# Router of a conditioned low-rank expert layer: four quarter products of TensorE side by side, gates turned on two column tiles

## The chip, the core and the metric

The kernel runs on one core of a Trainium2 chip. A core has five engines that run side by side and meet at semaphores: TensorE (PE in the profile; its weight loads are a row of their own, PEld), VectorE (DVE), ScalarE (ACT), GpSimd (POOL) and SyncE (SP, which here only issues DMAs). TensorE holds one operand (the weights, `lhsT`) in its array and streams the other (`rhs`) through it; results land in PSUM, 128 partitions by eight banks of 512 float32. The array can be used whole (128x128) or as smaller tiles, chosen by the partitions from which the operands come (rows of the array) and to which the result goes (columns). The metric is the device time of one execution, in microseconds (us). The profile's time is that of one execution taken by the hardware profiler.

## What is computed

`x` is 64 batches of 64 channels by 1024. Each batch picks one of 16 weight matrices (64x64) and mixes its channels by it; the mixed rows (4096 rows of 1024) go through a layer of 64 experts of rank 16, of which each row uses the 16 with the highest router scores. All is float32.

```python
W = weights[condition]                            # (64, 64, 64)
y = jnp.einsum('bct,bcd->bdt', x, W)              # mixed rows
xf = y.reshape(-1, 1024)
scores = xf @ Wr.T                                # (4096, 64)
top_vals, top_idx = jax.lax.top_k(scores, 16)
gates = jax.nn.softmax(top_vals, axis=-1)
G = jnp.zeros((N, K)).at[rows, top_idx].set(gates)
h = jnp.einsum('nd,krd->nkr', xf, A)
out = jnp.einsum('nkr,kdr->nd', h * G[:, :, None], B)
x = x + (out * 2.0).reshape(x.shape)
```

## The kernel before

The 4096 rows are handled in eight groups of 512 rows (`NG = 8`), each of four row tiles of 128 (`TPG = 4`); a row tile holds two batches of 64 rows. Since mixing the channels and multiplying by `A` commute, the kernel first multiplies the unmixed rows by `A` with the router's weights `Wr` appended (the products named `h_...`), and mixes afterwards with the 64x64 matrices `w_st` that GpSimd gathers per batch (`gather`). The mixed, gated result `hb` is multiplied by `B` (the products named `o_...`), and the input is added.

Both large products are done by a scheme with seven products instead of eight per level, two levels deep. The unit of the program's order is a *parent*, one of the seven outer products (p1 to p7); `run` writes one parent's work out by hand: inner products p1, p2, then the previous parent's p3, its own p6, the previous parent's p4, then the hooks `mid`, the operand sums for the next parent, the hooks `late`, then p7 and p5, then the hooks `end`. Each inner product is two matmuls of 272 columns (h) or 256 (o), in the profile four records. Inner products pile up in three PSUM banks a parent, x, y and w; ScalarE copies the pile x out three or four times while it grows (tiles `l_r1`, `l_a`, `l_b` at L601, and L608), and VectorE adds y and w. TensorE may go on with pile x only when ScalarE has copied it.

The first group does not use the inner level (lines L545, 512 columns), and its router scores come another way: `scores_t` (line tile `st`) multiplies `Wr` by the rows, with weights of 64 columns on two column tiles in turn, `turn` (`sp`) turns them, and `scores` mixes them from the tile `zr`. For groups 1 to 7 the scores before mixing are the last 16 columns of each quarter of z.

The router's steps of a group are hooks between products of other work:

- `scores` (L204 to L230): for each row tile i and batch j of it, one 64x64 weight block `ws[g][r, i, :]`, rows and result both on partitions `r`, that is, the upper-left or the lower-right quarter of the array. In group 0 one matmul of 64 columns each (L212, 8 of them), in the others two of 32 columns each (L221, 16). All results go into one PSUM tile `sw`, which one ScalarE copy (L229) takes to `sc`.
- `route_top` (VectorE, top 8 of each row at L243, and the negated maximum), `exps` (ScalarE, L249), `rest` (VectorE, the other 8, the mask, the sum and its reciprocal `inv`).
- `scaled` (L285 to L295): ScalarE multiplies the masked exponentials by `inv` into four tiles `g2`, each 128 rows by 2x64: the gates are written twice, side by side.
- `gates` (L297 to L302): TensorE transposes the four tiles (128x128 each) into the PSUM tile `gp`, and one ScalarE copy of 128x512 takes it to `gg`: experts on partitions, in both halves, rows of the group along the free axis.
- `gated` (L308 to L336): the mixing of h. Per quarter of z, 64 matmuls with 64x64 weights and 64 columns, each on another quarter of the array than the one before, the two row halves into two PSUM tiles `zp`; VectorE multiplies them by `gg` into `hb` (L334).

For groups 1 to 7 `scores` is a `mid` hook of the second parent after the group's last h parent, and `route_top` comes `late` in the same parent. In groups 2 to 6 `scaled` is a `mid` hook and `gates` a `late` hook of one parent, so TensorE has nothing of its own between them. In groups 1 and 7 `gates` is an `end` hook, so p7 and p5 of the parent stand between. In group 0 `scaled` ends one parent, and `gates`, directly followed by `gated`, is the `mid` hook of the next. PSUM tiles come from one pool of eight buffers (`acc`); every parent of groups 1 to 7 takes three, `sw` one, `gp` one, each `gated` two.

Of the kernel before, what the change touches and what calls it, by code (L numbers as in the profile page):

```python
# [9 lines left out]
F32 = mybir.dt.float32  # L10
# [5 lines left out]
P = 128  # L16
# [4 lines left out]
TPG = 4  # L21
CH = 4
HN = TPG * P // 2
HALF = BANK // 2
# [5 lines left out]
def kernel(  # L30
# [26 lines left out]
    nc = tc.nc  # L57
    N, T = x.shape
    B = cond.shape[1]
    C, D = N // B, cw.shape[1]  # L60
    KR = b_t.shape[0] * b_t.shape[3] * b_t.shape[2]
    K = wr_t.shape[2]
# [10 lines left out]
    small = ctx.enter_context(tc.tile_pool(name="small", bufs=2))  # L73
    acc = ctx.enter_context(tc.tile_pool(name="acc", bufs=8, space=PSUM))
# [66 lines left out]
    ident = const.tile([P, P], F32)  # L141
# [9 lines left out]
    ws = {}  # L151
# [17 lines left out]
    gg = blocks.tile([P, TPG * P], F32, name="gg")  # L169


    def scores_t(st):

        g = st["g"]
        s = acc.tile([P, 2, HN], F32, tag="acc", name=f"st_{g}")
        for h in range(2):
            for c in range(2 * CH):
                e = slice((c % 2) * K, (c % 2 + 1) * K)
                nc.tensor.matmul(
                    s[e, h, :],  # L180
                    lhsT=wr_sb[:, c, :],
                    rhs=xq[g, c // CH, h][:, c % CH, :],
                    start=(h == 0 and c < 2),
                    stop=(c >= 2 * CH - 2),
                    skip_group_check=True,
                )
        st_sb = mp0.tile([P, 2, BANK], F32, tag="m", name=f"st_sb_{g}")[:, 0, :]
        nc.scalar.copy(st_sb, s.rearrange("p h n -> p (h n)"))
        st["st"] = st_sb
# [13 lines left out]

    def scores(st):  # L204

        g = st["g"]
        sw = acc.tile([P, TPG, K], F32, tag="acc", name=f"sw_{g}")
        for i in range(TPG):
            for j in range(2):
                r = slice(j * C, (j + 1) * C)  # L210
                if "zr" in st:
                    nc.tensor.matmul(  # L212
                        sw[r, i, :],
                        lhsT=ws[g][r, i, :],
                        rhs=st["zr"][r, i, :],
                        start=True,
                        stop=True,
                    )
                    continue
                for k in range(2):  # L220
                    nc.tensor.matmul(  # L221
                        sw[r, i, ts(k, K // 2)].rearrange("p (d k) -> p d k", d=2),
                        lhsT=ws[g][r, i, :],
                        rhs=halves(st["z"][i // 2, k])[r, i % 2, :, HALF:],
                        start=True,
                        stop=True,
                    )
        scs = small.tile([P, TPG, K], F32, tag="sc", name=f"sc_{g}", bufs=1)
        nc.scalar.copy(scs, sw)  # L229
        st["sc"] = scs  # L230

    def route_top(st):
# [52 lines left out]
    def scaled(st):  # L285
        st["g2"] = []
        for i in range(TPG):
            g2 = small.tile([P, 2, K], F32, tag=f"g2_{i}", name=f"g2_{st['g']}_{i}", bufs=1)
            nc.scalar.activation(
                g2,  # L290
                st["e"][:, i, :].unsqueeze(1).to_broadcast([P, 2, K]),
                AF.Copy,
                scale=st["inv"][:, i : i + 1],
            )
            st["g2"].append(g2)  # L295

    def gates(st):  # L297

        gp = acc.tile([P, TPG, P], F32, tag="acc", name=f"gp_{st['g']}")
        for i in range(TPG):  # L300
            nc.tensor.transpose(gp[:, i, :], st["g2"][i].rearrange("p a k -> p (a k)"), ident)  # L301
        nc.scalar.copy(gg.rearrange("p (i n) -> p i n", n=P), gp)  # L302

    def halves(m):

        return m.rearrange("p s (d k) -> p s d k", d=2)
# [551 lines left out]
    for k, g in (  # L858
# [4 lines left out]
        st = sts[g]  # L863
# [79 lines left out]
    st = sts[0]  # L943
    h, o = st["h"], st["o"]
# [11 lines left out]
    a_sums(2)  # L956
    at(h + 1, "mid", a_sums, 3)
    at(h + 1, "end", scores_t, st)
    at(h + 1, "end", sums, st, "x_sums", "s3")
    at(h + 2, "mid", turn, st)  # L960
    at(h + 2, "mid", a_sums, 4)
    at(h + 2, "end", scores, st)
    for j in ("p1", "p2"):
        at(h + 2, "end", steps_of, first_steps[j], 1)
    at(h + 3, "mid", route_top, st)
    at(h + 3, "mid", sums, st, "x_sums", "s4")
    at(h + 3, "end", exps, st, 0, 1, 2, 3)
    at(h + 4, "mid", rest, st, 0, 1, 2, 3)
    at(h + 4, "end", scaled, st)
    at(h + 4, "end", b_sums, 1)  # L970
    at(h + 5, "mid", gates, st)
    at(h + 5, "mid", gated, st, 0, 0)
    at(h + 5, "end", b_sums, 2)
# [39 lines left out]
    for st in sts[1:]:  # L1013
        n, g = st["h"] + 7, st["g"]
        at(n + 1, "mid", scores, st)
        at(n + 1, "late", route_top, st)
        at(n + 2, "mid", exps, st, 0, 1)
# [20 lines left out]
        for i, (k, when) in enumerate(slots):  # L1038
            at(n + k, when, rest, st, i)
        at(n + scale[0], scale[1], scaled, st)  # L1040
        at(n + turned[0], turned[1], gates, st)
        for (k, when), *quarters in pairs:
            for i, j in quarters:
# [4 lines left out]
    for st in sts:  # L1048
        g, h, o = st["g"], st["h"], st["o"]
# [71 lines left out]
```

## Time and profile before

| what | value |
|---|---|
| median of 3 runs | 781.17 us (780.6 to 781.56) |
| the profiled execution | 780.21 us |
| its span, from first to last instruction | 778.4 us (1.8 us lie around it) |
| granted TensorE clock | 0.999 |
| TensorE busy | 770.6 us, 99% of the span |
| VectorE busy | 623.8 us, 80% |
| ScalarE busy | 184.5 us, 24% |
| GpSimd busy | 73.8 us, 9% |
| mean share of the 16 DMA engines, 300 to 695 us | 0.78 |
| `scores`, groups 1 to 7 (L221): matmul records | 224 |
| `gates`, all groups (L301): matmul records | 32 |
| copy of `sw` to `sc` (L229) | 372 ns, 8 times |
| copy of `gp` to `gg` (L302) | 585 ns, 8 times |

A matmul's record in the profile runs from its start to a modelled end, and neighbours overlap; a float32 product shows as two records, a transpose as one. What a stage costs on TensorE is therefore read from the chain of waits, where each piece begins when the one before it has ended.

### The profile page before, as it was taken

Reading aid. Unit: us, or ns where it says so; the run is one execution under the profiler, and the core shown is the slowest. Engines: PE = TensorE matmul, PEld = TensorE weight load, DVE = VectorE, ACT = ScalarE, POOL = GpSimd, SP = SyncE. Lnnn points to the kernel's source line nnn. Section 1 sums busy time; section 2 is a strip of 40 time slices with the busy share of each in tenths; the row PEclk is TensorE's granted clock in tenths of the full one; section 3 lists DMA queues with packets and bytes.
Section 4 is the critical chain, followed back from the end, with each engine's and each line's share of the span. In section 5 each row is a group of like instructions: output and inputs, shape, how many; then the busy total and the mean of one; then the engine's idle time right before and its main releaser. Section 6 shows DMA issues by size and latency. Waiting matters only on the chain.

```text
span 778.4 us, 14669 instructions
## 1 busy us (share of the span) xinstructions
PE 770.6 (99%) x5348; PEld 610.9 (78%) x5348; DVE 623.8 (80%) x1310; ACT 184.5 (24%) x490; POOL 73.8 (9%) x103
## 2 busy tenths in 40 slices
PE   9999999999999999999999999999999999999997
PEld 4445448888888888887888888888888888888886
DVE  4789867678889878897788976889768888688987
ACT  1120002223122222222222222222222231222221
POOL 4235352000200020000200010000200000000000
PEclk9999999999999999999999999999999999999999
DMA  9959678656788768896788958799488893687997
GB/s 331 399 182 332 264 248 300 211 157 238 226 272 298 264 220 287 281 304 226 244 284 278 319 194 283 258 294 330 137 313 268 283 355 113 229 257 250 341 383 259
DMA packets 107607, 208.50 MB, mean 268 GB/s; under 512 B 11072, under 2 KB 27200, under 8 KB 106640
## 3 DMA queue, kind: packets, MB, share of 16 engines
q1 hardware_dynamic: 100496, 186.83, 70.6%
q0 software_dynamic: 6608, 19.95, 7.4%
q8 instruction: 43, 0.70, 0.4%
q10 hardware_dynamic: 432, 0.79, 0.3%
q14 instruction: 28, 0.23, 0.1%
HBM read 174.41 MB, written 33.11 MB: 267 GB/s over the span
## 4 chain that ended last, share of the span: by engine, by line
PE 95%; DVE 3%; DMA 1%; issue 0%; ACT 0%; ACTq 0%; DVEq 0%
PE h_p_x L508 23%; PE o_p_x L508 20%; PE h_p_w L508 12%; PE o_p_w L508 10%; PE h_p_y L508 6%; PE o_p_y L508 5%; PE zp L321 4%; PE o_x L545 4%; PE h_x L545 3%; PE h_w L545 2%; PE o_w L545 2%; DMA x<-in_x_t_dram 1%; DVE o L87 1%; PE sw L221 1%; PE gp L301 1%; PE h_y L545 1%
## 5 line engine op out<-in xcount | busy, mean ns | idle before, releaser
L508 PE MATMUL o_p_x<-lo_p_p,l_t 128*128 128x256 f32 x584 | 142.9, 379 | 0.0
L508 PEld LDWEIGHTS o_p_x<-lo_p_p,l_t 128*128 128x128 f32 x584 | 111.0, 190 | 15.4
L87 DVE TENSOR_TENSOR o<-o,m_o_p 128x1024 f32<-128x1024 f32 x65 | 78.0, 1219 | 0.6
L157 POOL DMA_INDIRECT w_st<-in_cw_dram,idx x32 | 34.9, 1089 | 429.1 <-PE zp L321 412.9
L87 DVE TENSOR_TENSOR m_h_p<-h_p_w,l_a 128x272 f32<-128x272 f32 x49 | 21.6, 440 | 62.6 <-PE h_p_w L508 60.3
L87 DVE TENSOR_TENSOR m_h_p<-m_h_p,m_h_p 128x1088 f32<-128x1088 f32 x49 | 62.3, 1284 | 0.2
L508 PE MATMUL h_p_x<-a,l_t 128*128 128x272 f32 x224 | 60.5, 392 | 0.0
L508 PE MATMUL h_p_w<-lh_p_p,l_t 128*128 128x272 f32 x196 | 53.8, 397 | 0.0
L508 PE MATMUL h_p_x<-lh_p_p,l_t 128*128 128x272 f32 x196 | 52.9, 392 | 0.0
L508 PE MATMUL o_p_w<-lo_p_p,l_t 128*128 128x256 f32 x196 | 51.1, 383 | 0.0
L508 PEld LDWEIGHTS h_p_x<-a,l_t 128*128 128x128 f32 x224 | 42.6, 190 | 8.6
L601 ACT COPY l_b<-h_p_x 128x272 f32<-128x272 f32 x49 | 18.9, 385 | 121.9 <-PE h_p_x L508 117.2
L334 DVE TENSOR_TENSOR hb<-zp,gg 128x512 f32<-128x512 f32 x64 | 39.9, 684 | 7.0 <-PE zp L321 7.0
L508 PE MATMUL h_p_x<-at,l_t 128*128 128x272 f32 x168 | 45.4, 392 | 0.0
L508 PEld LDWEIGHTS h_p_x<-lh_p_p,l_t 128*128 128x128 f32 x196 | 37.2, 190 | 7.5
L601 ACT COPY l_b<-o_p_x 128x256 f32<-128x256 f32 x49 | 18.2, 372 | 103.8 <-PE o_p_x L508 103.8
L508 PEld LDWEIGHTS h_p_w<-lh_p_p,l_t 128*128 128x128 f32 x196 | 36.5, 191 | 7.0
L508 PEld LDWEIGHTS o_p_w<-lo_p_p,l_t 128*128 128x128 f32 x196 | 36.6, 190 | 5.2
L87 DVE TENSOR_TENSOR m_o_p<-o_p_w,l_a 128x256 f32<-128x256 f32 x48 | 20.3, 423 | 22.5 <-PE o_p_w L508 22.5
L321 PEld LDWEIGHTS zp<-w_st,m_h_p 64*64 64x64 f32 x2048 | 31.7, 135 | 7.9 <-issue 7.7
L508 PEld LDWEIGHTS h_p_x<-at,l_t 128*128 128x128 f32 x168 | 31.9, 190 | 6.6
L608 ACT COPY m_h_p<-h_p_x 128x272 f32<-128x272 f32 x49 | 18.9, 385 | 70.7 <-PE h_p_x L508 70.7
(174 smaller groups left out, 1387.3 us busy)
## 6 DMA issues: line engine op xcount, KB each, us to landing
lo_p_p<-o_p_p SPq DMA_DIRECT2D x280, 256.0 KB, 3.7
lh_p_p<-h_p_p SPq DMA_DIRECT2D x147, 272.0 KB, 5.4
lo_p_p<-in_b_t_dram SPq DMA_DIRECT2D x63, 256.0 KB, 4.5
x<-in_x_t_dram SPq DMA_DIRECT2D x31, 512.0 KB, 5.4
o<-in_x_dram SPq DMA_DIRECT2D x28, 512.0 KB, 7.2
out_dram<-o SPq DMA_DIRECT2D x27, 512.0 KB, 5.7
o_p_p<-os_p_p POOLq DMA_DIRECT2D x28, 256.0 KB
b<-in_b_t_dram SPq DMA_DIRECT2D x4, 1024.0 KB, 17.9
```

Source lines behind the costliest of these rows:

```text
L87: nc.vector.tensor_tensor(o, a, b, ALU.add)
L157: nc.gpsimd.indirect_dma_start(out=w_st[:, i, :], out_offset=None, in_=cw, in_offset=bass.IndirectOffsetOnAxis(ap=idx[:, n : n + 1], axis=0),)
L221: nc.tensor.matmul(sw[r, i, ts(k, K // 2)].rearrange("p (d k) -> p d k", d=2), lhsT=ws[g][r, i, :], rhs=halves(st["z"][i // 2, k])[r, i % ...
L301: nc.tensor.transpose(gp[:, i, :], st["g2"][i].rearrange("p a k -> p (a k)"), ident)
L321: nc.tensor.matmul(zp[b][e * D : (e + 1) * D, c, s, :], lhsT=halves(z)[r, s, c // 2, ds(c % 2 * P + e * D, D)], rhs=ws[g][r, 2 * i + s, :] ...
L334: nc.vector.tensor_tensor(tokens(hb[j, i])[:, :, :, b, :], zp[b], g_ij[:, :, :, b, :], ALU.mult)
L508: nc.tensor.matmul(bank, lhsT=v[:, c, :], rhs=w[:, c, :width], start=first and c == 0, stop=c == 1, skip_group_check=True,)
L545: nc.tensor.matmul(piles[n, s], lhsT=left()[j][:, c, ts(s, P)], rhs=w, start=c == 0 and PILES[kind][j].isupper(), stop=c == CH - 1, skip_g ...
L601: nc.scalar.copy(par["val"][n], par["bank"]["x"])
L608: nc.scalar.copy(before["q"][0][1], before["bank"]["x"])
```

## The change

`scores` now writes two PSUM tiles, one for each half of the array's rows (batch b of the row tile), and sends the result of odd row tiles to the other half of the partitions: `ROWS[b ^ (i % 2)]`. In this way the four products of a pair of row tiles stand on the four quarters of the array. The loops are reordered so that they follow each other: pair of row tiles, half of the columns, row tile, batch. The number of matmuls and their sizes stay. Four ScalarE copies of 64 partitions by 2x64 instead of one of 128x256 take the scores to `sc`, and put those that stand in the wrong half in place.

`scaled` writes the gates once (128x64), not twice. `gates` turns each of the four tiles by a matmul with the identity (weights 128x64, 128 columns) instead of a transpose, even row tiles to the lower half of the partitions, odd ones to the upper half of `gp`, which shrinks to 128x256. Four ScalarE copies of 64 partitions by 2x128 instead of one of 128x512 write both halves of `gg` from it.

```diff
+    ROWS = (slice(0, C), slice(C, P))
...
     def scores(st):
         g = st["g"]
-        sw = acc.tile([P, TPG, K], F32, tag="acc", name=f"sw_{g}")
-        for i in range(TPG):
-            for j in range(2):
-                r = slice(j * C, (j + 1) * C)
...
-                for k in range(2):
-                    nc.tensor.matmul(
-                        sw[r, i, ts(k, K // 2)].rearrange("p (d k) -> p d k", d=2),
-                        lhsT=ws[g][r, i, :],
-                        rhs=halves(st["z"][i // 2, k])[r, i % 2, :, HALF:],
...
+        sw = [acc.tile([P, TPG, K], F32, tag="acc", name=f"sw_{g}_{b}") for b in range(2)]
+        def product(b, n, i, rhs):
+            o = sw[b][ROWS[b ^ (i % 2)], i, n]
+            if len(rhs.shape) == 3:
+                o = o.rearrange("p (d k) -> p d k", d=2)
+            nc.tensor.matmul(o, lhsT=ws[g][ROWS[b], i, :], rhs=rhs, start=True, stop=True)
+        for m in range(TPG // 2):
+            for k in range(1 if "zr" in st else 2):
+                for i in (2 * m, 2 * m + 1):
+                    for b in range(2):
+                        if "zr" in st:
+                            product(b, slice(0, K), i, st["zr"][ROWS[b], i, :])
+                        else:
+                            z = halves(st["z"][m, k])[ROWS[b], i % 2, :, HALF:]
+                            product(b, ts(k, K // 2), i, z)
         scs = small.tile([P, TPG, K], F32, tag="sc", name=f"sc_{g}", bufs=1)
-        nc.scalar.copy(scs, sw)
+        for i in range(2):
+            for b in range(2):
+                nc.scalar.copy(scs[ROWS[b], i::2, :], sw[b][ROWS[b ^ i], i::2, :])
...
     def scaled(st):
-            g2 = small.tile([P, 2, K], F32, tag=f"g2_{i}", name=f"g2_{st['g']}_{i}", bufs=1)
+            g2 = small.tile([P, K], F32, tag=f"g2_{i}", name=f"g2_{st['g']}_{i}", bufs=1)
             nc.scalar.activation(
                 g2,
-                st["e"][:, i, :].unsqueeze(1).to_broadcast([P, 2, K]),
+                st["e"][:, i, :],
...
     def gates(st):
-        gp = acc.tile([P, TPG, P], F32, tag="acc", name=f"gp_{st['g']}")
+        gp = acc.tile([P, TPG // 2, P], F32, tag="acc", name=f"gp_{st['g']}")
         for i in range(TPG):
-            nc.tensor.transpose(gp[:, i, :], st["g2"][i].rearrange("p a k -> p (a k)"), ident)
-        nc.scalar.copy(gg.rearrange("p (i n) -> p i n", n=P), gp)
+            nc.tensor.matmul(
+                gp[ROWS[i % 2], i // 2, :], lhsT=st["g2"][i], rhs=ident, start=True, stop=True
+            )
+        gg_ = gg.rearrange("p (m i n) -> p m i n", i=2, n=P)
+        for i in range(2):
+            for r in ROWS:
+                nc.scalar.copy(gg_[r, :, i, :], gp[ROWS[i], :, :])
```

## The prediction, made before the changed kernel ran

> **What bounds the kernel now.** I read the busy times first, then what TensorE waited for, then the chain of waits around each place that the change touches, and last the timeline there. From the page, and from the waits of TensorE over the whole span (engine, line, releaser: us in total, times, longest):
>
> ```profile
> PE 770.6 (99%) x5348; PEld 610.9 (78%) x5348; DVE 623.8 (80%) x1310; ACT 184.5 (24%) x490; POOL 73.8 (9%) x103
> PE 95%; DVE 3%; DMA 1%; issue 0%; ACT 0%; ACTq 0%; DVEq 0%
> ```
>
> ```profile
> PE o_p_w L508 <- DVE o L87: 0.9, 1, 0.9
> PE h_w L545 <- DVE m_h_p L87: 0.7, 1, 0.7
> ```
>
> TensorE is busy almost without a gap and the chain runs on it for 95%, so what its queue gains or loses moves the end. The exceptions are group 0 (the 0.7 at h_w), group 7's router, where the chain runs on VectorE, and the last 13 us. The chain (start, length, piece, records) at `scores` in groups 0 and 1, at `st`, at `gates` in groups 1 and 2, and at mixings:
>
> ```profile
> 20.23 3.60 PE st L179 x32
> 23.84 3.63 PE h_w L545 x8
> 31.79 0.61 PE sw L212 x16
> 50.21 1.09 PE zp L321 x64
> 62.80 3.43 PE o_x L545 x8
> 167.90 0.92 PE h_p_w L508 x4
> 168.81 1.07 PE sw L221 x32
> 169.89 1.11 PE h_p_w L508 x4
> 191.17 0.44 PE gp L301 x4
> 191.60 0.92 PE h_p_x L508 x4
> 196.19 2.02 PE zp L321 x128
> 263.46 1.06 PE gp L301 x4
> ```
>
> The reader is to see three things. The mixing `zp`, on all four quarters, needs (2.02-1.09)/64 = 14.5 ns a record, and 1.09-64x0.0145 = 0.16 us to get going; `sw`, on two quarters, (1.07-0.16)/32 = 28.4 ns a record, `sw` of group 0 with twice the columns (0.61-0.16)/16 = 28.1. Half the quarters, half the rate, whatever the columns. Second, four whole-array records that follow a tiled stage take 1.11 instead of 0.92: 0.19 for going back, about the 0.190 of one 128x128 weight load; h_w after `st` shows it too (3.63 against 3.43). Third, `gp` takes 0.44 in group 1 and pays nothing before or behind, since a transpose uses the whole array; in group 2 it takes 1.06. Why, the timeline says:
>
> ```profile
> 262.86 1.28 ACT L289 ACTIVATE g<-es,invs 128x128 f32<-128x128 f32 x4
> 264.19 0.14 PEld L301 LDWEIGHTS gp<-ident,g 128*128 128x128 f32 x1 [0.15 <-ACT g L289]
> 264.55 0.58 ACT L302 COPY gg<-gp 128x512 f32<-128x512 f32 x1 [0.42 <-PE gp L301]
> 266.39 0.39 ACT L601 COPY l_b<-h_p_x 128x272 f32<-128x272 f32 x1 [1.25 <-PE h_p_x L508]
> ```
>
> There each turn waits for ScalarE's `g2`, one per 0.30 us. So do groups 3 to 7 (1.06 each, 1.21 in group 7).
>
> **Scores, groups 1 to 7.** Same 32 records, on four quarters: 0.16+32x0.0145 = 0.62 instead of 1.07, 0.45 less; the 0.19 behind it stays. 7x0.45 = -3.1. That the quarters change with each product is no news to TensorE: `zp` does the same at 14.5. The bounds are 14.5 and the present 28.4 (nothing gained); I take 14.5, since it is the same weights, the same array and the same rotation. The Trainium skill has a floor that speaks against this (TensorE: Matmul & The Clock Gate, section "Wait — 56ns, not 53.3ns?"): starts of matmuls never closer than about 25 ns, however small. By it a stage would take 0.96; the trace does not agree, its `zp` records follow at 14.5.
>
> **Group 0.** `sw` gains 16x13.6 ns = 0.22; `gates` there pays 0.16 to get going (`zp` behind it pays its way back already). Both lie ahead of h_w at 55.66, which waits 0.7 for VectorE, itself held by a store's DMA (0.36 idle at 54.32). So 0; without that cover -0.06.
>
> **Gates.** Four transposes (four records) become four matmuls with 64 weight columns, eight records of 128 columns. o_x gives 3.43/8 = 429 ns for 512 columns, so 107 for 128. That two column tiles run at once `st` shows: (3.60-0.16)/32 = 107 ns for 256 columns, half of the 214 that one alone needs. Eight records: 8x107/2 = 0.43, as now; but getting going 0.16 and going back 0.19 come on top. Group 1: +0.34. The Trainium skill warns of this (TensorEngine Tiling, section "Key Properties"): changing the tiling mode, not merely the tile, drains TensorE. The trace agrees, 1.11 against 0.92; without it, the gates would be free here.
>
> Groups 2 to 7: `g2` shrinks from 128 to 64 columns. `es` of that size took 1.06 for four (337 ns each), `g` 1.28, so the last `g2` is ready 0.22 earlier. Behind it stood one record (0.11), with the next weights already on their way; now two records (0.21) and the way back (0.19): +0.30-0.22, I take +0.1 each, 6x0.1 = +0.6. Bounds: -0.12 if the next weights are still loaded ahead, +0.34 if the earlier `g2` brings nothing; -0.7 to +2.1 in all. In group 7 the chain comes down VectorE from 697.37 to the `g2` at 711.31, but it begins there with a wait for TensorE (0.89 idle), so what `scores` gains at 690 moves it along.
>
> **ScalarE.** Its copies took 585 ns for 512 elements and 372 for 256: 0.83 ns an element, 0.27 us for 128. Four for `sc` take at most 1.06 us instead of 0.37, four for `gg` at most 4x0.372 = 1.49 instead of 0.585. What hides the first, in group 3:
>
> ```profile
> 314.46 0.37 ACT L229 COPY sc<-sw 128x256 f32<-128x256 f32 x1 [1.57 <-PE sw L221]
> 316.38 0.37 ACT L601 COPY l_b<-o_p_x 128x256 f32<-128x256 f32 x1 [1.55 <-PE o_p_x L508]
> ```
>
> ```profile
> 315.19 0.60 DVE L243 MAX8 tops<-sc 128x8 f32<-128x64 f32 x4
> 316.78 0.42 DVE L87 TENSOR_TENSOR m_o_p<-o_p_w,l_b 128x256 f32<-128x256 f32 x1 [0.79 <-ACT l_b L601]
> ```
>
> `sw` ends 0.45 earlier, at about 314.0, so the copies end by 315.1, ahead of MAX8 (which now waits for two of them) by 0.1 and of `l_b` by over 0.8. If they are later, MAX8 and the add of pile w queued behind it slide into the 0.79 that VectorE idles. `gg` would end by 264.6+1.5 = 266.1, ahead of `l_b` (266.39) and of the first `hb` that reads it (267.48). In group 7 `l_r` behind it slides from 713.88 to some 714.5; TensorE needs it two products and a p3 later, at 715.6. So 0; with the cover gone, each 0.1 us late would cost 0.7 over the groups.
>
> **PSUM.** `sw` takes a second of the eight buffers, so the parents behind it get others. In the order as built this only adds waits of TensorE for its own products of a parent or more before; the present ones of that kind stand in pieces that show 0.92. So 0.
>
> **Sum.** -3.1+0.34+0.6 = -2.2: 780.21 becomes 778.0 in the profiled execution, whose span holds all of this. The median of the runs stands 0.96 above that execution, so 781.17-2.2 = 779.0. The terms' bounds give -3.1+0.34-0.7 = -3.5 to -3.1+0.34+2.1 = -0.7, 777.7 to 780.5.
>
> **Rivals.**
> - *Gates at full price* (0.12): the earlier `g2` buys nothing and each turn pays 0.34. -3.1+7x0.34 = -0.7, 780.5. For it: the order of the turns is bound to ScalarE's. Against: one record per `g2` leaves TensorE idle 0.15 of each 0.30.
> - *Gates free* (0.07): the way back hides in the wait; 777.7. For: the next weights are loaded during the last turn now. Against: they aren't after `st` or `zp`.
> - *A floor per record* (0.08): the 28 ns are not two quarters at work but the step at which TensorE starts such records. Then `scores` gains nothing and the gates' 0.34+0.6 = 0.94 is all that is left: 781.17+0.9 = 782.1, within 0.2%. For: 28.4 and 28.1 for 32 and 64 columns. Against: 14.5 in `zp`. By the skill's floor, cited above, it would be 781.3.
> - *Slower* (0.11): the quarter changes with every product (before with every second), and if the 0.135 us weight load of each is exposed, a stage takes 0.16+16x0.135 = 2.3, +1.25x7 = +8.7, with the gates 781.17+9.6 = 790.8. It decides against the change from 24 ns a record on, where the gates' 0.94 is no longer covered ((1.07-0.94/7-0.16)/32), and is seen as slower from 31. Against: `zp` again; for: its operand is contiguous, that of `scores` 2x16 columns, 272 apart.
>
> **Chances.** The forecast has 0.62. A measurement of this kernel can tell 0.2% (1.6 us) from no change. Faster by more: nearly all of the forecast (0.58) and the free gates, 0.65. Within: the rest of the forecast, full price and floor, 0.24. Slower: 0.11. The range is that of the bounds with the runs' own spread of 0.4 on either side, 777.3 to 780.9; it leaves out the floor and the slower case.
>
> **What would show it.** In the new chain: `sw` 0.62 with 32 records and 1.11 (1.06 for o) behind it; `gp` eight records, in group 1 about 0.6 with 1.11 behind it, in groups 2 to 6 no more than 1.06 to the end of its turns and 0.19 behind; VectorE's MAX8 without a wait for ScalarE, `l_b` still waiting for TensorE. The forecast is wrong if `sw` stays above 0.8, if `gp` with what follows grows by over 0.4, or if TensorE shows waits for ScalarE's copies that are not there now.

## The result, and the profile after

The changed kernel takes 778.33 us (median of 7 runs, 777.96 to 779.44), the kernel before on the same chip 780.49 (7 runs, 780.25 to 781.56): a ratio of 0.9969, 95% interval 0.9959 to 0.9978, or 2.4 us less (2.2 by the two medians). Timed once more beside other kernels it came to 778.73 against 780.78, 0.9972 (0.9960 to 0.9983). The forecast was 779.0 and 2.2 us less; the 0.7 us between 779.0 and 778.33 is that of its base, 781.17 from three runs of the kernel before where seven give 780.49.

The profiled execution of the changed kernel is the slowest of its seven: 779.44 us, and its span, 777.7 us, is only 0.7 us shorter than that of before. So the profiles must be compared stage by stage. The busy times from its page, and then the chain of waits (start, length, piece, records) at the places that were shown of before:

```profile
PE 768.8 (99%) x5380; PEld 609.4 (78%) x5380; DVE 623.8 (80%) x1310; ACT 195.2 (25%) x538; POOL 73.8 (9%) x103
```

```profile
169.45 0.60 PE sw L216 x32
170.05 1.11 PE h_p_w L515 x4
...
191.33 0.59 PE gp L303 x8
191.92 1.11 PE h_p_x L515 x4
...
263.49 0.95 PE gp L303 x7
264.44 1.11 PE h_p_w L515 x4
...
729.10 1.78 PE zp L328 x108
730.88 1.42 issue
732.30 0.56 PE zp L328 x17
```

`sw` fell from 1.07 to 0.60, in every group from 1 to 7. The starts of its single records in the trace show how: before, two records start every 58 ns, one for each quarter at work, now four do, and a mixing starts four every 58 ns too. `gp` in group 1 grew from 0.44 to 0.59, and the four records behind it from 0.92 to 1.11: the way to the column tiles and the way back. (The records of `gp` start in pairs, 0.11 us apart, so 0.43 of the 0.59 is the four pairs themselves.) In group 2 (and alike to group 6) `gp` itself is 0.11 shorter and the piece behind it 0.19 longer. The last three lines are new: in the last mixing TensorE stands still for 1.42 us in the middle of its own stream, waiting for nothing that the profile shows.

ScalarE around the gates of group 2, and around the scores of group 3, in the timeline of the changed kernel:

```profile
262.89 1.06 ACT L290 ACTIVATE g<-es,invs 128x64 f32<-128x64 f32 x4
264.37 0.76 PEld L515 LDWEIGHTS h_p_w<-lh_p_p,l_t 128*128 128x128 f32 x4 [0.17 <-issue]
264.48 1.50 ACT L309 COPY gg<-gp 64x256 f32<-64x256 f32 x4 [0.52 <-PE gp L303]
266.51 0.39 ACT L608 COPY l_b<-h_p_x 128x272 f32<-128x272 f32 x1 [0.53 <-PE h_p_x L515]
```

```profile
314.12 1.10 ACT L230 COPY sc<-sw 64x128 f32<-64x128 f32 x4 [1.10 <-PE sw L216]
315.31 0.60 DVE L244 MAX8 tops<-sc 128x8 f32<-128x64 f32 x4
```

The four `g2` take 1.06 instead of 1.28. The next whole-array weights (264.37) are no longer loaded ahead: PEld stood idle 0.17 before them. The four copies cost 1.50 us and 1.10 us end to end, and still end ahead of `l_b` (which waits for TensorE as before) and, by 0.09 us, of MAX8 (VectorE's waits list none for these copies in any group).

Added up from the two profiles (each number a piece of the chain, after minus before, in us):

| term | forecast | measured |
|---|---|---|
| scores, groups 1 to 7: 7 x (0.60-1.07) | -3.1 | -3.29 |
| gates, group 1: (0.59+1.11)-(0.44+0.92) | +0.34 | +0.34 |
| gates, groups 2 to 6: 5 x ((0.95+1.11)-(1.06+0.92)); group 7: (1.15+1.06)-(1.21+0.87) | +0.6 | +0.40+0.13 |
| the stages together | -2.2 | -2.42 |
| start of group 0's h_w: 56.30-55.66 | 0 | +0.64 |
| a pause in a mixing: 1.74 after, 0.68 before | not foreseen | +1.06 |
| all | -2.2 | -0.72 (spans: -0.7) |

The pause is what a mixing with its interruption takes beyond the usual 2.02: 1.78+1.42+0.56-2.02 = 1.74. The kernel before has one too, in group 3's first mixing, of 2.02+0.36+0.32-2.02 = 0.68, as its chain shows; the forecast had passed over these lines:

```profile
360.35 2.02 PE zp L321 x126
362.37 0.36 issue
362.73 0.32 PE zp L321 x2
```

The stages alone come to the runs' 2.4, but the runs can hold pauses too; the last two terms are needed for the profiled pair. What they are the experiments had to tell. (One number told above of the kernel before is wrong: a quarter's mixing in `gated` is 32 matmuls, 64 records, and a pair of quarters the 128 records of one `zp` piece.)

### The profile page after: what moved, and what is told of

The parts are those of the page before. It is cut to its first block, busy times and chain, and to the rows that moved or that the text cites. A ratio compares the mean times of both kernels' runs of the same rounds, so it can differ in the third digit from the quotient of the medians.

```text
span 777.7 us, 14792 instructions
## 1 busy us (share of the span) xinstructions
PE 768.8 (99%) x5380; PEld 609.4 (78%) x5380; DVE 623.8 (80%) x1310; ACT 195.2 (25%) x538; POOL 73.8 (9%) x103
## 4 chain that ended last, share of the span: by engine, by line
PE 89%; issue 4%; DVE 3%; POOL 2%; DMA 1%; ACT 0%; POOLq 0%; DVEq 0%
PE h_p_x L515 23%; PE o_p_x L515 20%; PE h_p_w L515 12%; PE o_p_w L515 10%; PE h_p_y L515 6%; PE o_p_y L515 5%; PE zp L328 4%; PE o_x L552 4%; PE o_w L552 2%; POOL w_st L157 1%; DMA cond_b<-in_cond_dram 1%; DVE o L87 1%; PE h_w L552 1%; PE o_y L552 1%; PE gp L303 1%
```

## The experiments

**The scores alone.** The new `scores`; `scaled` and `gates` as in the kernel before.

```diff
-            g2 = small.tile([P, K], F32, tag=f"g2_{i}", name=f"g2_{st['g']}_{i}", bufs=1)
+            g2 = small.tile([P, 2, K], F32, tag=f"g2_{i}", name=f"g2_{st['g']}_{i}", bufs=1)
...
+            nc.tensor.transpose(gp[:, i, :], st["g2"][i].rearrange("p a k -> p (a k)"), ident)
+        nc.scalar.copy(gg.rearrange("p (i n) -> p i n", n=P), gp)
```

> The new scores with the gates of before. Theory (the parts add up, and TensorE's queue sets the end): the scores stage 0.60 us on the chain as in the changed kernel, gp back at 0.44 in group 1 and 1.06 in groups 2 to 6 with 0.92 behind it; 7 x (1.07-0.60) = 3.3 us less than before, about 777.2. Rival (the changed kernel's gain owes something to the gates too, by the earlier g2): no more than 2.4 us less. Rival on group 0 (the four copies of the scores push VectorE's work there): h_w again starts at about 56.3 us instead of 55.7 and eats 0.6 of the gain.

776.87 us against 781.02, a ratio of 0.9948 (0.9935 to 0.9962): 4.1 us less, 3.0 to 5.1, so the 3.3 of the theory is inside and the rival's 2.4 is not. In its chain the scores take 0.60, `gp` 0.44 in group 1 and 1.06 in groups 2 to 6, and the pause is back where before has it, behind 125 records of group 3's first mixing. h_w starts at 56.17; whether that comes of the scores is taken up below.

**The gates alone.** The new `scaled` and `gates`; `scores` as in the kernel before.

```diff
-        sw = [acc.tile([P, TPG, K], F32, tag="acc", name=f"sw_{g}_{b}") for b in range(2)]
+        sw = acc.tile([P, TPG, K], F32, tag="acc", name=f"sw_{g}")
...
+        nc.scalar.copy(scs, sw)
```

> The new gates with the scores of before. Theory: slower by the way to and from the column tiles, +0.34 in group 1, +0.08 in groups 2 to 6, +0.13 in group 7, together 0.9 us, about 781.4 (a ratio of 1.001, at the edge of what is measured). Rival (gates free or better, since g2 comes 0.22 earlier): 780.5 or less. Rival on group 0 (the four copies of the gates push the work there): h_w at 56.3 us here and not with the scores alone.

781.94 us against 781.02, a ratio of 1.0017 (1.0008 to 1.0026): 1.3 us more, 0.6 to 2.0. The gates cost; the rival, for which they were free, is out, and by the stages too, which are those of the changed kernel (0.59 and 0.95, 1.11 behind), +0.87 in all by the table. The last mixing has a pause again, behind 111 records, of 1.78+0.90+0.50-2.02 = 1.16 us, where the kernel before has 0.68 elsewhere. So a pause in the last mixing comes with the new gates, not with the new scores. h_w starts at 56.05, earlier than with the scores alone, so the rival on group 0 has nothing for it either.

**The old order on four quarters.** The changed kernel with the loops of `scores` in the order of before.

```diff
-        for m in range(TPG // 2):
-            for k in range(1 if "zr" in st else 2):
-                for i in (2 * m, 2 * m + 1):
-                    for b in range(2):
+        for i in range(TPG):
+            for b in range(2):
+                for k in range(1 if "zr" in st else 2):
```

> The changed kernel with the old order of the products in the scores (row tile, batch, half of the columns), still on four quarters. Theory (the quarters count, the order doesn't, since TensorE loads weights ahead): 0.60 us a stage, as in the changed kernel. Rival (two products in a row on one quarter hold up the queue): between 0.62 and 1.07, with 1.07 if the order does everything.

**Two quarters in the new order.** The changed kernel with the results of odd row tiles in their own half.

```diff
-            o = sw[b][ROWS[b ^ (i % 2)], i, n]
+            o = sw[b][ROWS[b], i, n]
...
-                nc.scalar.copy(scs[ROWS[b], i::2, :], sw[b][ROWS[b ^ i], i::2, :])
+                nc.scalar.copy(scs[ROWS[b], i::2, :], sw[b][ROWS[b], i::2, :])
```

> The changed kernel with the products of odd row tiles sent back to their own half, so that only two quarters of the array work, in the new order, two PSUM tiles and four copies as in the changed kernel. Theory (quarters at work set the rate): 1.07 us a stage again. Rival (the new order gives the gain): 0.60.

The scores stage of group 1 in the chain of each, first the old order on four quarters, then the new order on two:

```profile
169.32 0.63 PE sw L216 x32
```

```profile
168.98 1.05 PE sw L216 x32
```

The quarters do it. The order is worth 0.03 us a stage, whichever way it is turned: 0.60 or 0.63 on four quarters, 1.05 or 1.07 on two. That the results go to two PSUM tiles and are copied in four pieces does not do it, since the run with 1.05 has both. (One run each: 779.26 and 781.60 us; both pause behind record 108 of the last mixing, as the changed kernel does, for 1.44 and 1.19 us.)

**Pair turns.** The changed kernel's scores and copies, but the gates of two row tiles side by side in one tile, turned by one whole-array transpose; the result stands in `gp` exactly where the changed kernel puts it.

```diff
-        for i in range(TPG):
-            g2 = small.tile([P, K], F32, tag=f"g2_{i}", name=f"g2_{st['g']}_{i}", bufs=1)
+        for m in range(TPG // 2):
+            g2 = small.tile([P, 2, K], F32, tag=f"g2_{m}", name=f"g2_{st['g']}_{m}", bufs=1)
+            for i in range(2):
+                nc.scalar.activation(
+                    g2[:, i, :],
+                    st["e"][:, 2 * m + i, :],
...
-            nc.tensor.matmul(
-                gp[ROWS[i % 2], i // 2, :], lhsT=st["g2"][i], rhs=ident, start=True, stop=True
-            )
+        for m in range(TPG // 2):
+            nc.tensor.transpose(gp[:, m, :], st["g2"][m].rearrange("p a k -> p (a k)"), ident)
```

> The new scores; the gates of two row tiles lie side by side in one tile and are turned by one whole-array transpose, two per group instead of four turns, into the same places of gp. Theory: no way to and from column tiles, so 0.92 (0.86) behind gp; gp 0.22 us in group 1 and, in groups 2 to 6, last g2 0.22 earlier with one record behind it, about 0.84 instead of 1.06. Against before: -3.3 (scores) -0.2 (group 1) -6 x 0.2 (groups 2 to 7) = -4.7, about 775.8; against the changed kernel -2.3. Rival (the drain around gp isn't from the column tiles but from waiting on ScalarE's tiles): 1.11 behind gp stays and the gain over the changed kernel is under 1.0.

776.72 against 781.02, 0.9947 (0.9933 to 0.9960). Its chain at the gates of groups 1 and 2, and at group 5's first mixing:

```profile
190.87 0.22 PE gp L304 x2
191.09 0.92 PE h_p_x L514 x4
```

```profile
262.99 0.33 PE gp L304
263.32 0.92 PE h_p_w L514 x4
```

```profile
545.09 2.02 PE zp L327 x127
547.11 0.89 issue
548.00 0.21 PE zp L327
```

The drain around `gp` does come of the column tiles: with whole-array transposes 0.92 stands behind it in both groups. From the scores to the first mixing of group 2 it takes 265.15-218.84 = 46.31 us, 46.61 in the changed kernel and 46.53 with the scores alone, so the pair turns gain 0.3 a group on the changed kernel, as expected. The time is 4.1 us under before (3.1 to 5.2), so the expected 4.7 is inside, but by its median it is hardly better than the scores alone (776.72 against 776.87): here a pause of 2.02+0.89+0.21-2.02 = 1.10 us stands at the very end of a mixing, in yet another group (0.53 with the scores alone).

**Both kernels once more.** The kernel before and the changed kernel, unchanged, one profile each.

> The kernel before, unchanged, profiled once more. Two pieces of its chain are in question. If h_w of group 0 starts at 55.7 us here too, its later start with the changed kernel (56.3) comes of the change; if it lies anywhere from 55.6 to 56.4, it is the loading of that execution. If the pause inside a mixing (0.36 us idle after 126 of 128 records, in group 2) stands at the same record again, it belongs to a place in the program; if it moves to another mixing or is gone, it is chance alone.

> The changed kernel, unchanged, profiled once more. By the theory that a place in the program decides: a pause again after some 108 of 128 records of the last mixing, though its length may differ (1.42 us in the first profile). By chance alone: elsewhere or none. Group 0's h_w: 56.3 again if the change moves it, otherwise anywhere from 55.6 to 56.4.

The kernel before (781.03 us) pauses again behind record 126 of the same mixing (at 360, which is group 3's, not 2's as the expectation has it), for longer:

```profile
360.96 2.02 PE zp L321 x126
362.98 0.55 issue
363.53 0.33 PE zp L321 x2
```

The changed kernel (778.94 us) pauses again behind record 108 of the last mixing, 0.87 us idle instead of 1.42 (1.19 us in all). So the place belongs to the program, the length to the execution. And h_w of group 0: 56.27 here with the kernel before, 56.34 with the changed one. The first profile's 55.66 was an early case of a start that lies between 55.66 and 56.54 in the eleven profiles with 10 idle matmuls. Two profiles of the kernel before (55.66, 56.27) and three of the changed one (56.30, 56.34, 56.05) show no hand of the change in it; what moves it stays open.

**The instructions shifted.** The changed kernel with 16 idle matmuls at the start instead of 10.

```diff
-    for _ in range(10):
+    for _ in range(16):
         nc.tensor.matmul(idle, lhsT=ident, rhs=ident, start=True, stop=True)
```

> The changed kernel with 16 instead of 10 idle matmuls at the start, where TensorE waits for the first rows anyway. Each is two records, that is four instructions with the weight loads, so every later instruction of TensorE stands 24 places further on. If the pause in the last mixing comes where a 16 KB block of TensorE's instructions ends and the next has not arrived, it moves 12 records ahead, from about 108 to about 96. If it comes of the data or of the moment, it stays at 108 or is gone. The scores and gates stages: unchanged.

The last mixing in its chain:

```profile
728.70 1.56 PE zp L328 x96
730.26 1.56 issue
731.82 0.69 PE zp L328 x29
```

The pause moved from record 108 to record 96, by the 12 records that the 24 instructions make. It hangs on the instruction's place in the program, not on the data or the moment. The trace has TensorE's instructions one by one (weight loads, matmuls, and a record for each separate wait). Counted there, the paused records of all twelve profiles with a pause (126 before, 125 with the scores alone, 108, 111 with the gates alone, 96, 127 with the pair turns) stand at one and the same remainder of 256. And the page of the changed kernel has a queue that loads instructions (number of pieces, MB, share of the DMA engines):

```profile
q8 instruction: 43, 0.70, 0.4%
```

That is 16.3 KB a piece, some 64 bytes for each of TensorE's 11,133 records in that trace, 256 to a piece. The Trainium skill describes such blocks (Runtime: NRT & Kernel Launch, section "Instruction fetch mechanics": a FIFO refilled by the sequencer in 16 KiB blocks of 256 instructions) and says that crossing one is mostly hidden. Mostly, the trace agrees; here, where a mixing goes through 256 instructions in 2.0 us, a crossing cost between 0.5 and 1.8 us in each profile but one.

That TensorE waits there for its instructions the trace shows as well, since it has the time of every piece. In the changed kernel one began to load at 729.81 and had landed at 730.80; TensorE stopped at 730.88 and went on at 732.30. In all twelve cases TensorE went on 2.2 to 2.5 us after such a piece had begun, 1.2 to 1.5 us after it had landed. With pieces and block ends counted in order, the thirteen profiles have 546 pairs. In just twelve the piece began less than 2.0 us before the last record ahead of the block's end, and these are the twelve pauses, from 1.56 us idle where it began 0.5 us before to 0.20 where it began 2.0 us before. At 2.1 us two of three ends cost 0.2 each (one with 16 idle matmuls, at 199.8 us, and one with the pair turns, below); from 2.2 us on no end shows a delay.

**The place chosen.** The pair turns with 8 idle matmuls, which puts the end of the block behind group 5's first mixing; beside it the pair turns as above and the changed kernel, all on one chip.

```diff
-    for _ in range(10):
+    for _ in range(8):
```

> The kernel with the new scores and pair turns, with 8 instead of 10 idle matmuls at the start, so that TensorE's instructions stand 8 places (4 records) earlier. Theory (a block of 256 instructions ends after 127 of 128 records of group 5's first mixing there and the next one is late): the block's end falls behind that mixing and the pause of 0.9 us at 547 is gone from the profile; about 0.9 us less than with 10 idle matmuls, near 775.8 against 776.7. Rival (the pause is a matter of the moment): a pause somewhere else or there, and no difference in time.

> The kernel with the new scores and pair turns again, beside the one with 8 idle matmuls on one chip: by the theory of the place the pause stands again after 127 of 128 records of group 5's first mixing, at 0.9 us or so, and the time is again about 4.3 us under before.

> The changed kernel, timed beside the two with pair turns on one chip: 2.2 us under before as measured so far; the pair turns 2.3 us under it by their stages (gates 0.3 us a group in groups 1 to 7).

| kernel | median of runs (us) | ratio to before (780.78) | 95% interval | pause in its profile (us) |
|---|---|---|---|---|
| pair turns, 8 idle | 774.65 (5) | 0.9919 | 0.9906 to 0.9933 | none |
| pair turns, 10 idle | 776.49 (5) | 0.9939 | 0.9926 to 0.9953 | 2.02+0.62+0.21-2.02 = 0.83, and 0.20 at 362 us |
| changed kernel | 778.73 (7) | 0.9972 | 0.9960 to 0.9983 | 1.78+0.87+0.56-2.02 = 1.19 |

Group 5's first mixing in the chain with 8 idle matmuls:

```profile
545.15 2.02 PE zp L327 x128
```

The pause is gone and none has come elsewhere. The block now ends three records behind that mixing, 2.2 us after its piece began. Between the two pair turns the time fell by 1.8 us, twice the pause. In the profiled pair, 1.7 us apart, the rest has names: with 10 idle matmuls the block that ends behind group 3's first mixing costs 0.20 (`362.30 1.12 PE h_p_y L514 x4`, where 0.92 is usual), and h_w of group 0 starts at 56.54 instead of 55.91, but it started at 55.84 in the first profile with 10. Whether the runs without a profile differ by the same three pieces is not shown. This is the fastest version: 6.3 us under before (5.2 to 7.3), 4.1 under the changed kernel by the medians. The pair turns with 10 idle matmuls are 2.2 under it, where 2.3 was expected.

## Why the prediction was right

- *TensorE's queue sets the end*: right. The stages sum to -2.42; with the 0.6 that the pauses take on top (below) it is -1.8. Both lie in the measured 1.7 to 3.2 us less. That the two medians differ by the forecast 2.2 is partly luck: the stages gave 0.2 more than forecast, and the pauses took some back.
- *Scores 0.62 a stage*: 0.60, that is (0.60-0.16)/32 = 13.8 ns a record instead of 14.5. That half the quarters give half the rate was shown by the two orders and the two counts of quarters. It holds for 64 columns as for 32: in group 0 `sw` fell from 0.61 to 0.39 (in the profile with 16 idle matmuls, `32.95 0.39 PE sw L216 x16`), that is, from 28.1 to 14.4 ns a record, and so by the 0.22 forecast. The 13.8 also settles the rivals of a floor per record and of exposed weight loads, which needed 24 ns and more.
- *Gates pay for the way there and back where nothing covers it*: right to 0.01 us in group 1 (+0.34). Under ScalarE's `g2` the way there is covered, the earlier `g2` gives back 0.11 and the way back costs 0.19: +0.08 a group where +0.1 was forecast (and 0.13 in group 7). The upper bound of these six groups, 6x0.34, is 2.0 and not the 2.1 of the sum, which hardly moves the range. Neither "full price" (+0.34) nor "free" came; the gates alone made the kernel slower, and pair turns took the 0.19 away again.
- *ScalarE's eight copies cost nothing*: right, but close: the four copies for `sc` took 1.10 us, over the "at most 1.06", since back to back they don't overlap at all, and MAX8's margin was 0.09 us.
- *Group 0 comes to nothing*: right as far as is shown, but the row behind it, h_w at 55.66, was one execution's value of something that moves by 0.9 us.
- *PSUM costs nothing*: TensorE's waits list no new one for a buffer, and the places with the additional waits keep their 0.92.
- *What the prediction did not have*: that 64 more instructions for the gates' float32 products (and a few separate waits) shift every later instruction of TensorE, and so the place where a block of 256 ends. Before, one ended 2 records ahead of the end of a mixing (0.68 and 0.88 us in two profiles); after, 20 ahead of the end of the last (1.74, 1.19, 1.19). That is about 0.6 us lost by the means of these (1.37 against 0.78; the other runs have no profile), a term that the sum lacked and the range covered. In the first profiled pair it took 1.06 and h_w's start 0.64, which is why that pair shows 0.7 us less and the runs 2.4.

## What to carry to other kernels

Products of 64x64 weights and 32 or 64 columns ran here at the rate of the quarters that are at work, so sending alternate results to the other half and letting the copies put them in place pays where the copies are hidden; but a transpose turned into a product on column tiles pays for leaving and re-entering the whole array, and packing two narrow tiles side by side into one whole-array transpose gives the same layout for half the records and no switch. Where small products follow each other at some 8 ns an instruction, a few instructions added anywhere ahead can move a block's end into them and cost or give a microsecond: a difference of 0.1 to 0.2% between two versions should be read stage by stage before it is believed.

## What the runs showed of the hardware that was not expected

- Each quarter of the array started one record of a product with 64x64 weights every 58 ns, with 32 columns as with 64: two records in 58 ns on two quarters, four on four.
- TensorE stood idle for 0.2 to 1.56 us in the middle of a mixing at the end of a block of 256 of its instructions, at the same record in each execution of a program, with a length that changes; shifting the program by 24 instructions moved it by 12 records. It went on 2.2 to 2.5 us after the next piece of instructions had begun to load.
- Not every such end pauses. Each pair of quarters is just 256 instructions, so each of the 14 mixings of groups 1 to 7 has one. An end pauses when its piece began less than some 2 us before it, and there are two ways to that. In the kernel before the piece began 0.9 us after the block before had ended, near the median of all (1.0), but the block's instructions had all begun 2.65 us after that end. In the changed kernel they took 5.8 us, and the piece began only 5.0 us after the end before. Why it began so late is open: the DMA engines were busy for 0.97 of the stretch from 728 to 732 us there, and for 0.46 of that from 360 to 363 in the kernel before.
- A float32 transpose of 128x128 is one record of 0.11 us and leaves no trace in its neighbours (0.92 behind it in groups 1 to 6); four products on column tiles in its place, of the same 128 columns, add 0.16 ahead (0.59 less four pairs of records at 0.107) and 0.19 behind.
